# A fused attention kernel: order of additions, PSUM tiles and pieces of projection work rearranged

## The chip, the cores and the metric

The kernel runs on one core of a Trainium2 chip. TensorE (PE in the profile) multiplies matrices; PEld is its loading of weights. VectorE (DVE), ScalarE (ACT) and GpSimd (POOL) work on the results, and SyncE (SP) issues DMAs; ScalarE and GpSimd can issue some as well. Each engine takes its own instructions in order. The metric is device time in microseconds, and less is better. Times inside a run come from one profiled execution, counted from its first instruction.

## The reference

The input x holds 16 images of 256 channels and 32 x 32 pixels, so 1024 tokens of 256 channels each, all fp32. Two layers follow each other:

```python
# layer 0: 4 heads of 64
qkv = xs @ w_proj + b_proj                    # xs: 1024 tokens x 256
attn = softmax(q @ k.T * 64 ** -0.5)
x = attn @ v @ w_out + b_out + xs
# layer 1: 8 heads of 32
h = group_norm(x, gn1_w, gn1_b)               # 32 groups of 8 channels
attn = softmax(q @ k.T * 32 ** -0.5 + phys_bias)
x = x + attn @ v @ proj_w.T + proj_b
h = group_norm(x, gn2_w, gn2_b)
x = x + mlp_w2 @ gelu(mlp_w1 @ h + mlp_b1) + mlp_b2   # 256 -> 1024 -> 256
```

## The kernel before, in words

Everything is kept as channels x tokens, 128 channels to a tile, and a token block (TB) is 512 tokens. For each image `b` the loop runs the first attention (`attention_a`), then either the first MLP half of the image before (`hidden`, lines 784 to 796) or, for image 0, the q, k and v projections of image 1; then the first part of this image's own projections for the second attention (`qkv_1`), and the second attention (`attention_b`). Into the second attention the remaining work is strewn in pieces: the rest of its own projections (`own`), the second MLP half of the image before (`outputs`), and the q, k and v projections for the next image (`first`). Images 0 and 15 have no `outputs` or no `first`, so they have fewer pieces.

Softmax isn't normalised at once. Scores go from TensorE to PSUM, ScalarE takes their exponentials to SBUF (tiles `e`), TensorE multiplies these with v (`weigh`, tiles `acc`), and VectorE adds the exponentials up (tiles `es`). At the end of an item (a token block and a group of heads) a matmul with ones gives the denominators (`den`), ScalarE copies them out, a DMA spreads them over partitions, VectorE inverts them, two more DMA steps bring them back as rows, and VectorE scales the result. Then the output projection runs, `o` for the first attention and `j` for the second, and its sum with x gets the statistics of the next group norm.

PSUM has eight banks of 128 x 512 fp32. Six make three wide tiles of two banks, s0 to s2, which `wide` (line 232) gives out by least recent use; two are the single banks 0 and 1 (`bank`, line 238). While the first attention works at an odd item, s2 holds its accumulator; the set `kept` then takes s2 out of the rotation. At an even item the accumulator is in banks 0 and 1. In the second attention a unit covers two blocks of 128 keys: the first block's scores go to banks 0 and 1 and one wide tile, the second's to two wide tiles. Bank 0 also takes the unit's `acc`, and once in each image the v projection named `v[1]` (`early`, line 898). Whoever writes a tile next waits until its last reader is done.

The order of work on every engine is fixed when the program is built. A `yield` in an attention ends a step; after each step `run` (line 828) issues the pieces that `fill` names for that step and advances `later`, a list of functions that are due a number of steps on. A scheduler then orders the instructions of each engine; `tc.keep_in_program_order` holds some of them.

The places that the change touches are these. `load_rest` (line 138) issues small loads on SP: `bqk`, the bias of q, k and v, and `pb`, the bias of the second softmax. The first image's q and k projections run as `first_qk` (line 854), named by half of the channels, by k or q, and by token block. `weigh` of the first attention empties an accumulator with a ScalarE copy (L373) and a VectorE addition (L374) and says when s2 returns. `normalise` (line 382) takes a wide tile for `den`. In the second attention `add` issues the additions of `es` (L497), `weigh` empties `acc` by a copy (L520) or an addition (L522), and the loop from line 566 sets their order. `v` of `qkv` empties its tile with a multiply on VectorE (L721). `group_norm` (line 618) has three functions due some steps apart: `means`, `variances` (matmul `gm`) and `apply` (matmul `gv`, then `rstd`, L662, which empties it); norm h is the second one of an image and runs during the first attention of the next.

Of the kernel before, what the change touches and what calls it, by code (L numbers as in the profile page):

```python
# [8 lines left out]
F32 = mybir.dt.float32  # L9
# [5 lines left out]
P = 128  # L15
GROUPS = 32
EPS = 1e-5
HEADS0, D0 = 4, 64
HEADS1, D1 = 8, 32
TB = 512  # L20
# [34 lines left out]
def kernel(  # L55
# [21 lines left out]
    nc = tc.nc  # L77
    B, C, S = x.shape
    HID = mlp_w1T.shape[1]
    CC = C // P  # L80
    SB = S // P
    NT = S // TB
# [54 lines left out]

    def load_rest():
        bp = b_proj.rearrange("(g i t d) -> i t d g", i=2, t=3, d=D0)
        for t in (1, 0):  # L140
            for i in range(2):
                nc.sync.dma_start(bqk[i * D0 : (i + 1) * D0, t, :], bp[i, t])
        nc.sync.dma_start(pb, phys_bias.partition_broadcast(P))
        for i in range(2):
            nc.sync.dma_start(bqk[i * D0 : (i + 1) * D0, 2, :], bp[i, 2])
        for t, w in weights:
            nc.sync.dma_start(t, w)
# [53 lines left out]
def first_pass(ctx, tc, x, out, k):  # L201
# [120 lines left out]
    def attention_a(b, qT, kT, v, project):  # L322
        key, D, lag = f"a_{b}", D0, 2
        items = [(t, c) for t in range(NT) for c in range(CC)]
        units = [(i, kb) for i in range(len(items)) for kb in range(SB)]
        res = act.tile([P, CC, S], F32, tag="res", name=f"res_{key}")
        accs, held, sums = {}, {}, {}

        def scores(i, kb):
            t, c = items[i]  # L330
            if kb == 0 and i % 2:
                kept.add(2)
            s = wide(f"s_{key}_{i}_{kb}")
            for g in range(2):
                for h in range(0, P, HALF):
                    nc.tensor.matmul(  # L336
                        s[h : h + HALF, g, :],
                        kT[g * D : (g + 1) * D, c, kb * P + h : kb * P + h + HALF],
                        qT[g * D : (g + 1) * D, c, t * TB : (t + 1) * TB],
                        start=True,  # L340
                        stop=True,
                    )
            e = work.tile([P, 2, TB], F32, tag="e", name=f"e_{key}_{i}_{kb}", bufs=8)
            nc.scalar.activation(e, s, AF.Exp, scale=float(D) ** -0.5)  # L344
            return i, kb, e

        def weigh(i, kb, e):
            t, c = items[i]
            if kb == 0:
                if i % 2:  # L350
                    acc = wide(f"acc_{key}_{i}", 2)
                    accs[i] = [acc[:, h, :] for h in range(2)]
                else:
                    accs[i] = [bank(f"acc_{key}_{i}_{h}", h) for h in range(2)]
            for h in range(2):
                for g in range(2):
                    nc.tensor.matmul(  # L357
                        accs[i][h][g * D : (g + 1) * D, :],
                        v[h * HALF : (h + 1) * HALF, kb, c * 2 + g],
                        e[h * HALF : (h + 1) * HALF, g, :],  # L360
                        start=(kb == 0),
                        stop=(kb == SB - 1),
                    )
            if kb == 0:
                held[i] = e
                return
            if kb == 1:
                sums[i] = work.tile([P, 2, TB], F32, tag="es", name=f"es_{key}_{i}", bufs=4)
            nc.vector.tensor_add(sums[i], held[i] if kb == 1 else sums[i], e)  # L369
            if kb == SB - 1:  # L370
                r = res[:, c, t * TB : (t + 1) * TB]
                one, two = accs.pop(i)
                nc.scalar.copy(r, one)  # L373
                nc.vector.tensor_add(r, r, two)  # L374
                if i % 2:

                    later.after(2, lambda: kept.discard(2))
                if c == CC - 1:
                    later.after(2 if t < NT - 1 else 1, lambda: normalise(t))


        def normalise(t):
            half = TB // 2
            den = wide(f"den_{key}_{t}")[:, 0, :]
            for c in range(CC):
                for g in range(2):
                    for h in range(2):
                        j = (2 * g + h) * 32
                        nc.tensor.matmul(
                            den[j : j + 32, c * half : (c + 1) * half],  # L390
                            k["ones"][:, :32],
                            sums[t * CC + c][:, g, h * half : (h + 1) * half],
                            start=True,
                            stop=True,
                        )
            denominators(
                f"{key}_{t}", den_copy(f"{key}_{t}", den), CC * TB,
                (2, 5) if t < NT - 1 else (1, 1),
                lambda full: scale(t, full),
            )  # L400

            if t == 0 and handed:
                handed.pop()()

        def scale(t, full):
            r = res[:, :, t * TB : (t + 1) * TB]
            halves = [
                y.rearrange(form, c=CC, h=2)
                for y, form in ((r, "p c (h q) -> p c h q"), (full, "p (h c q) -> p c h q"))
            ]  # L410
            tc.keep_in_program_order(nc.vector.tensor_mul(halves[0], *halves))
            if t == NT - 1:
                later.after(4, lambda: project(t, res)())

        cols[0] = 32
        pending = []
        for n, u in enumerate(units):
            pending.append(scores(*u))
            if n == len(units) - 1:
                break  # L420
            if n >= lag:
                weigh(*pending.pop(0))
            yield
        while pending:
            weigh(*pending.pop(0))
            if not pending:


                cols[0] = P
                first_half = project(0, res)  # L430
                first_half((0,))
                yield
                first_half((1,))
                break
            yield
# [7 lines left out]
    def attention_b(b, qT, kT, v, project):  # L443
# [44 lines left out]
        def add(i, kb, es, block):  # L488
# [6 lines left out]
            for n in range(G // 2):  # L495
                d = sums[i][n]
                ins = nc.vector.tensor_add(d, es[n] if kb == 0 else d, es[2 * block + n])  # L497
                if block:
                    tc.keep_in_program_order(ins)

        def weigh(i, kb, es):
            t, c = items[i]
            acc = bank(f"acc_{key}_{i}_{kb}", 0)
            for m in range(2):
                for g in range(G):
                    nc.tensor.matmul(  # L506
                        acc[g * D : (g + 1) * D, :],
                        v[:, kb + m, c * G + g],
                        es[2 * m + g // 2][:, g % 2, :],
                        start=(m == 0),  # L510
                        stop=(m == 1),
                    )
            if t not in res:
                res[t] = act.tile(
                    [P, CC, TB], F32, tag="res1" if t == NT - 1 else "res",
                    name=f"res_{key}_{t}",
                )
            r = res[t][:, c, :]
            if kb == 0:
                nc.scalar.copy(r, acc)  # L520
            else:
                nc.vector.tensor_add(r, r, acc)  # L522
            if kb == SB - 2:
                later.after(1, lambda: normalise(i, r, i == len(items) - 1))
# [41 lines left out]
        for u in units:  # L566
            now = scores(*u)
            add(*now, 0)
            if pending:
                weigh(*pending)  # L570
            add(*now, 1)
            pending = now
            yield
# [192 lines left out]
    def attention_1(b, qkv_tiles, xb, norm):  # L766
        q, kk, v = qkv_tiles
        stats = small.tile([P, CC, NT, 6], F32, tag="st1", name=f"st1_{b}", bufs=2)

        def project(t, res):  # L770
            return out_proj(
                f"j{b}", k["wpj"],
                lambda kc: res[:, kc, :],
                k["pjb"], xb, t, stats, (lambda: norm(stats)) if t == NT - 1 else None,
            )

        return attention_b(b, q, kk, v, project)
# [73 lines left out]
    xs = {0: load_x(0)}  # L851
    k["load_rest"]()
    tiles0, (first_qk, first_v) = qkv_0(0, xs[0])
    run_pieces(first_qk + first_v)
    k["exp_bias"]()


# [16 lines left out]
    for b in range(B):  # L874
# [34 lines left out]
            now, end = outputs[:5], outputs[5:]  # L909
        if not first:  # L910

            fill = {0: own[:2], 1: own[2:3], 2: own[3:5], 3: own[5:6], 4: own[6:]}
            fill.update({5 + 2 * m: [piece] for m, piece in enumerate(now)})
            now = []

        rest = [[piece] for piece in now]
# [7 lines left out]
        for m, pieces in enumerate(rest):  # L924
# [4 lines left out]
                b, tiles1, xs[b],  # L929
                lambda st, b=b, hn=hn: group_norm(  # L930
                    f"h{b}", xs[b], st, k["g2w"], k["g2b"], "q1", hn,
                    4 if b + 1 < B else 2, b == B - 1,
                ),
            ),
            fill,
# [305 lines left out]
```

## Time and profile before

| | |
|---|---|
| three timed runs, us | 3809.84, 3809.48, 3809.69 (median 3809.69) |
| the profiled run, us | 3809.61 |
| matmul groups, second attention: scores L467, weigh L506 | 535.4 us and 492.1 us busy |
| matmul groups, first attention: scores L336, weigh L357 | 530.9 us and 527.6 us busy |
| additions es_b L497 (all but each item's first) | 768 x 1219 ns |
| exponentials e_b L482 | 1280 x 865 ns in the mean |
| multiply that empties v_b, L721 | 64 x 684 ns |
| granted TensorE clock | 1.000 |

Busy times of different engines overlap, so they don't add up to the span. A line of the timeline gives start, length, engine, source line, operation, output and inputs, shape and count, and in brackets how long the engine had been idle and what ended that. A line of the waits gives who waited for whom, then the total in us, the number of times, and the longest. One fp32 matmul is two records, and matmuls that use different parts of the array start together: four of 128 x 32, or of 64 x 64, or eight of 32 x 64.

### The profile page before, as it was taken

What the parts mean: (1) busy time and instruction counts of PE and PEld (TensorE: products, weight loads), DVE (VectorE), ACT (ScalarE), POOL (GpSimd) and SP (SyncE); (2) the same over time, 40 slices, a digit from 0 to 9 for tenths busy, and PEclk for the clock granted to TensorE, in tenths of its full rate; (3) what the DMA queues carried; (4) which work ended last, traced back from release to release, by engine and by line L of the source; (5) the groups of instructions that cost most, each with busy time, mean ns of one, the idle gap of its engine ahead of it and who ended that gap; (6) DMA issues with size and microseconds to landing.
All of it is one profiled execution on the core that took longest, in us unless ns stands there. A gap on an engine that the chain in (4) does not pass through costs nothing.

```text
span 3807.8 us, 86808 instructions
## 1 busy us (share of the span) xinstructions
PE 3757.8 (99%) x38335; PEld 1490.8 (39%) x38335; DVE 2230.3 (59%) x2764; ACT 2034.1 (53%) x2624; POOL 79.0 (2%) x245
## 2 busy tenths in 40 slices
PE   9999999999999999999999999999999999999999
PEld 4333333333333333333333333333333333333335
DVE  4674646646566465665656656565565655646573
ACT  4555546555465554545546455554555545555462
POOL 1000000000000000000000000000000000000000
PEclk9999999999999999999999999999999999999999
DMA  2000000000001000000000001010000100000000
GB/s 84 12 13 12 30 12 16 27 12 30 12 16 32 7 30 12 19 29 7 30 12 23 25 10 32 7 33 15 13 30 7 33 15 13 30 7 22 15 13 21
DMA packets 63052, 78.27 MB, mean 21 GB/s; under 512 B 35820, under 2 KB 37356, under 8 KB 62668
## 3 DMA queue, kind: packets, MB, share of 16 engines
q1 hardware_dynamic: 60684, 71.85, 6.1%
q8 instruction: 302, 4.95, 0.5%
q0 software_dynamic: 400, 0.41, 0.1%
q14 instruction: 82, 0.67, 0.1%
q10 hardware_dynamic: 1584, 0.39, 0.0%
HBM read 54.28 MB, written 17.56 MB: 19 GB/s over the span
## 4 chain that ended last, share of the span: by engine, by line
PE 94%; DVE 2%; ACT 2%; issue 2%; DMA 0%; ACTq 0%; POOLq 0%; POOL 0%; DVEq 0%
PE s_b L467 13%; PE acc_b L506 12%; PE m L787 12%; PE m L279 12%; PE s_a L336 11%; PE acc_a L357 10%; PE qk_a L279 6%; PE qk_b L279 5%; PE o L279 3%; PE v_a L279 3%; PE j L279 3%; PE v_b L279 2%; PE den_b L531 1%; ACT e_b L482 1%; DVE es_b L497 1%
## 5 line engine op out<-in xcount | busy, mean ns | idle before, releaser
L482 ACT ACTIVATE e_b<-s_b 128x1024 f32<-128x1024 f32 (+1 forms) x1280 | 982.6, 865 | 500.0 <-PE s_b L467 500.0
L497 DVE TENSOR_TENSOR es_b<-es_b,e_b 128x1024 f32<-128x1024 f32 x768 | 899.6, 1219 | 365.6 <-ACT e_b L482 365.6
L344 ACT ACTIVATE e_a<-s_a 128x1024 f32<-128x1024 f32 x512 | 521.0, 1024 | 361.5 <-PE s_a L336 341.5
L467 PE MATMUL s_b<-q,k 32*64 32x512 f32 x8192 | 535.4, 601 | 30.2 <-DVE v L721 24.6
L336 PE MATMUL s_a<-q,k 64*64 64x512 f32 x4096 | 530.9, 592 | 3.3 <-ACT e_a L344 3.3
L357 PE MATMUL acc_a<-e_a,v 64*64 64x512 f32 x4096 | 527.6, 589 | 0.0
L369 DVE TENSOR_TENSOR es_a<-es_a,e_a 128x1024 f32<-128x1024 f32 x384 | 469.0, 1221 | 88.2 <-ACT e_a L344 76.0
L506 PE MATMUL acc_b<-e_b,v 128*32 128x512 f32 x4096 | 492.1, 598 | 0.0
L279 PE MATMUL m<-g,w 128*32 128x256 f32 (+1 forms) x7664 | 464.2, 379 | 0.0
L787 PE MATMUL m<-gn_h,w 128*128 128x512 f32 x1024 | 451.3, 595 | 0.3 <-DVE gn_h L677 0.3
L795 ACT ACTIVATE g<-m,m1b 128x512 f32<-128x512 f32 x256 | 175.9, 687 | 355.3 <-PE m L787 355.3
L279 PEld LDWEIGHTS m<-g,w 128*32 128x32 f32 (+1 forms) x7664 | 276.7, 112 | 217.2 <-issue 42.1
L467 PEld LDWEIGHTS s_b<-q,k 32*64 32x64 f32 x8192 | 172.5, 130 | 317.6 <-issue 149.5
L787 PEld LDWEIGHTS m<-gn_h,w 128*128 128x128 f32 x1024 | 192.2, 190 | 230.6 <-issue 229.8
L357 PEld LDWEIGHTS acc_a<-e_a,v 64*64 64x64 f32 x4096 | 160.1, 133 | 279.3 <-issue 242.4
L336 PEld LDWEIGHTS s_a<-q,k 64*64 64x64 f32 x4096 | 153.1, 133 | 276.8 <-issue 216.2
L506 PEld LDWEIGHTS acc_b<-e_b,v 128*32 128x32 f32 x4096 | 108.5, 109 | 351.6 <-ACT e_b L482 194.7
L522 DVE TENSOR_TENSOR res_b<-res_b,acc_b 128x512 f32<-128x512 f32 x192 | 130.9, 682 | 192.9 <-PE acc_b L506 192.9
L279 PE MATMUL qk_b<-gn_g,wq 128*32 128x512 f32 (+1 forms) x1280 | 234.0, 592 | 0.0
L279 PE MATMUL qk_a<-x,wp 128*32 128x512 f32 (+1 forms) x1856 | 231.0, 592 | 1.1 <-DMA x<-in_x_dram 1.0
L721 DVE TENSOR_TENSOR v<-v_b,eones 128x512 f32<-128x512 f32 x64 | 43.8, 684 | 242.5 <-PE v_b L279 242.5
L497 DVE TENSOR_TENSOR es_b<-e_b,e_b 128x1024 f32<-128x1024 f32 x128 | 150.7, 1219 | 52.4 <-ACT e_b L482 52.4
(121 smaller groups left out, 2095.3 us busy)
## 6 DMA issues: line engine op xcount, KB each, us to landing
rd_a<-row_a SPq DMA_DIRECT2D x64, 256.0 KB
out_dram<-x SPq DMA_DIRECT2D x64, 256.0 KB
rd_b<-row_b SPq DMA_DIRECT2D x252, 64.0 KB
x<-in_x_dram SPq DMA_DIRECT2D x30, 512.0 KB
w<-in_L_conv_mlp_w_dram SPq DMA_DIRECT2D x2, 1024.0 KB
x<-in_x_dram SPq DMA_DIRECT2D x4, 256.0 KB
sp_b<-d_b SPq DMA_DIRECT2D x63, 8.0 KB
row_b<-inv_b SPq DMA_DIRECT2D x63, 8.0 KB
```

The costliest lines, as they stand in the source:

```text
L279: nc.tensor.matmul(o[sl], w[:, sl], r, **flags)
L336: nc.tensor.matmul(s[h : h + HALF, g, :], kT[g * D : (g + 1) * D, c, kb * P + h : kb * P + h + HALF], qT[g * D : (g + 1) * D, c, t * TB : ...
L344: nc.scalar.activation(e, s, AF.Exp, scale=float(D) ** -0.5)
L357: nc.tensor.matmul(accs[i][h][g * D : (g + 1) * D, :], v[h * HALF : (h + 1) * HALF, kb, c * 2 + g], e[h * HALF : (h + 1) * HALF, g, :], st ...
L369: nc.vector.tensor_add(sums[i], held[i] if kb == 1 else sums[i], e)
L467: nc.tensor.matmul(outs[g][h : h + HALF, :], kT[g * D : (g + 1) * D, c, k0 : k0 + HALF], qT[g * D : (g + 1) * D, c, t * TB : (t + 1) * TB] ...
L482: nc.scalar.activation(to, s, AF.Exp, scale=float(D) ** -0.5)
L497: ins = nc.vector.tensor_add(d, es[n] if kb == 0 else d, es[2 * block + n])
L506: nc.tensor.matmul(acc[g * D : (g + 1) * D, :], v[:, kb + m, c * G + g], es[2 * m + g // 2][:, g % 2, :], start=(m == 0), stop=(m == 1),)
L522: nc.vector.tensor_add(r, r, acc)
L787: nc.tensor.matmul(ps, k["w1"][:, cc, hc * P : (hc + 1) * P], hn[0][:, cc, t * TB : (t + 1) * TB], start=(cc == 0), stop=(cc == CC - 1),)
L795: nc.scalar.activation(g, ps, AF.Gelu, bias=k["m1b"][:, hc : hc + 1])
```

## The change

The change has these parts, in the order of the diff:

1. `pb` and the q and k parts of `bqk` are loaded from ScalarE's queue in place of SP's, `pb` first.
2. In the first attention s2 returns to the rotation inside `normalise`, after the denominators have taken their tile; before, it returned two steps after the accumulator was emptied, just ahead of the denominators. After the last item it returns at once. The denominators and the next projection so take each other's tiles.
3. In the second attention the results of image 0 (all but the last token block) lie in the MLP's tiles `g`, and those of image 15 in `q0`, a tile for each.
4. At the first unit of the second attention a `yield` comes between the two calls of `add`, so the pieces of step 0 are issued ahead of the first additions.
5. The first image's projections run with all pieces of the first token block first.
6. In images 0 and 15 `own` is given out one piece to a step, the v pieces first, and the output pieces follow two steps later than before.
7. `variances` of norm h is due after 3 steps in place of 4, except in the last image.

```diff
     def load_rest():
         bp = b_proj.rearrange("(g i t d) -> i t d g", i=2, t=3, d=D0)
+        nc.scalar.dma_start(pb, phys_bias.partition_broadcast(P))
         for t in (1, 0):
             for i in range(2):
-                nc.sync.dma_start(bqk[i * D0 : (i + 1) * D0, t, :], bp[i, t])
-        nc.sync.dma_start(pb, phys_bias.partition_broadcast(P))
+                nc.scalar.dma_start(bqk[i * D0 : (i + 1) * D0, t, :], bp[i, t])
...
                 nc.vector.tensor_add(r, r, two)
-                if i % 2:
-
-                    later.after(2, lambda: kept.discard(2))
+                if i == len(items) - 1:
+                    kept.discard(2)
...
                 lambda full: scale(t, full),
             )
 
+            kept.discard(2)
             if t == 0 and handed:
                 handed.pop()()
...
+        def result(t):
+            if t < NT - 1 and b == 0:
+                return [
+                    work.tile([P, TB], F32, tag="g", name=f"res_{key}_{t}_{c}", bufs=16)
+                    for c in range(CC)
+                ]
+            tag = "res1" if t == NT - 1 else "res" if b < B - 1 else "q0"
+            r = act.tile([P, CC, S if tag == "q0" else TB], F32, tag=tag, name=f"res_{key}_{t}")
+            return [r[:, c, :TB] for c in range(CC)]
...
             add(*now, 0)
-            if pending:
-                weigh(*pending)
+            if not pending:
+
+                yield
+                add(*now, 1)
+                pending = now
+                continue
+            weigh(*pending)
             add(*now, 1)
             pending = now
             yield
...
-    run_pieces(first_qk + first_v)
+
+    run_pieces(first_qk[::2] + first_qk[1::2] + first_v)
...
-            fill = {0: own[:2], 1: own[2:3], 2: own[3:5], 3: own[5:6], 4: own[6:]}
-            fill.update({5 + 2 * m: [piece] for m, piece in enumerate(now)})
+            fill = {m: [piece] for m, piece in enumerate(own[:5:2] + own[1::2] + own[6:])}
+            fill.update({len(own) + 2 * m: [piece] for m, piece in enumerate(now)})
...
-                    4 if b + 1 < B else 2, b == B - 1,
+                    3 if b + 1 < B else 2, b == B - 1,
```

More of the change, by code (lines that the diff above doesn't have):

```diff
@@ L513, in weigh @@
             if t not in res:
[L514 to L518, printed above, removed]
+                res[t] = result(t)
+            r = res[t][c]
             if kb == 0:
@@ L772, in project @@
                 f"j{b}", k["wpj"],
-                lambda kc: res[:, kc, :],
+                lambda kc: res[kc],
                 k["pjb"], xb, t, stats, (lambda: norm(stats)) if t == NT - 1 else None,
```

## The prediction

> **What bounds the kernel now.** I read the page first, then the waits of TensorE alone, then the timeline around each wait.
>
> ```profile
> span 3807.8 us, 86808 instructions
> PE 3757.8 (99%) x38335; PEld 1490.8 (39%) x38335; DVE 2230.3 (59%) x2764; ACT 2034.1 (53%) x2624; POOL 79.0 (2%) x245
> ...
> PE 94%; DVE 2%; ACT 2%; issue 2%; DMA 0%; ACTq 0%; POOLq 0%; POOL 0%; DVEq 0%
> ```
>
> TensorE is the bound: it is busy for 99% of the span and carries 94% of the chain that ended last. Only what shortens its work or its waits counts; vector and scalar work is free as long as nobody waits for it. The diff leaves the matmuls as they are, so the whole question is the waits. The waits of TensorE name them (total us, times, longest):
>
> ```profile
> PE s_b L467 <- DVE v L721: 24.6, 16, 1.5
> PE den_a L389 <- DVE res_a L374: 8.1, 16, 0.8
> PE s_b L467 <- DVE res_b L522: 4.4, 8, 0.9
> PE s_a L336 <- ACT e_a L344: 3.3, 15, 0.2
> ...
> PE s_b L467 <- ACT res_b L520: 1.0, 3, 0.7
> PE qk_a L279 <- DMA x<-in_x_dram: 1.0, 1, 1.0
> ```
>
> The first two come once per image, 16 times in all. These totals are too small: a matmul of 512 columns is shown as 0.59 us long, but the next may start 0.43 us after it (in the undisturbed timeline score and weigh groups start 0.86 us apart, each of two passes of 0.43). So I take waits from start to start. The biggest one, in image 5 (column one is the start, column two the length):
>
> ```profile
> 1270.15 1.93 PE L279 MATMUL v_b<-wq,gn_g 128*32 128x256 f32 x32
> 1271.90 1.90 PE L279 MATMUL qk_b<-gn_g,wq 128*32 128x512 f32 x16
> 1272.32 2.36 DVE L497 TENSOR_TENSOR es_b<-e_b,e_b 128x1024 f32<-128x1024 f32 x2 [3.27 <-ACT e_b L482]
> 1274.60 0.68 DVE L721 TENSOR_TENSOR v<-v_b,eones 128x512 f32<-128x512 f32 x1
> 1275.34 1.98 PE L467 MATMUL s_b<-q,k 32*64 32x512 f32 x32 [1.53 <-DVE v L721]
> ...
> 1280.71 1.90 PE L279 MATMUL qk_b<-gn_g,wq 128*32 128x512 f32 x16
> 1282.54 1.97 PE L467 MATMUL s_b<-q,k 32*64 32x512 f32 x32
> ```
>
> The projection qk_b has four groups of 0.43, so the scores could start at 1271.90 + 1.72 = 1273.62; they start at 1275.34, 1.72 late. They want bank 0, which v_b filled and the multiply L721 must empty; that multiply stands on VectorE behind two additions of 1.2 us, though its input was done at about 1272. The last two lines are the same pair of steps without a wait: 1282.54 against 1280.71 + 1.72 leaves 0.11 us, the price of the switch alone. So 1.72 - 0.11 = 1.61 us per image is wait.
>
> The second wait, in image 6:
>
> ```profile
> 1428.15 1.04 PE L357 MATMUL acc_a<-e_a,v 64*64 64x512 f32 x8
> 1428.93 0.68 DVE L374 TENSOR_TENSOR res_a<-res_a,acc_a 128x512 f32<-128x512 f32 x1
> 1429.67 1.07 PE L389 MATMUL den_a<-es_a,ones 128*32 128x256 f32 x16 [0.48 <-DVE res_a L374]
> 1430.56 3.62 PE L279 MATMUL j<-res_b,wpj 128*32 128x512 f32 x32
> ```
>
> The denominators could start at 1428.15 + 0.86 = 1429.01 and start 0.66 late, when L374 has emptied tile s2; net of the switch 0.55.
>
> **What the Trainium skill says.** "Perfetto Trace Analysis", section Optimization Strategy: a gap that repeats on the engine that should be full can mean that there is no free PSUM tile; both waits are exactly that. The same page, section Matmuls: independent groups should rotate through banks so that emptying one lies beside the next group; here bank 0 is given to v_b and then at once to the scores, and s2 from the accumulator to the denominators. "ScalarE: Activation LUTs", section What ACT_TABLE_LOAD costs, gives 1283 ns and a drain of about 1380 ns; the trace agrees on 1.28 us (10.60 to 11.88), but the first activation follows at 11.89, with no drain between. "DMA: Bandwidth & Descriptors", section Anatomy of one DMA: a DMA's semaphore wait is held by the issuing engine's sequencer. The trace agrees: SP issues its first bqk at 2.87 and its second only at 5.20.
>
> **The change part by part.** The order of the built program is what I follow.
>
> The order on VectorE: in all 16 images the multiply of v_b 1 now stands before the two additions. The cause is the yield between the first scores and their additions. In the 14 middle images nothing else moves there. v_b's last pass starts at about 1271.68; the earlier multiply (v_b 0) began 0.42 after its last pass started, so this one runs from 1272.1 to 1272.8, before 1273.62. The additions then start 0.5 us later than before, at 1272.8, and end at 1275.2; the next additions could then start at 1277.57 - 1.72 = 1275.85, so the delay is absorbed. ScalarE had done the first unit's exponentials by 1273.20 and its k copy runs 1273.87 to 1274.45; the second half of the scores, 1273.73 + 0.86 = 1274.59, is the first to want that tile. Gain 14 x 1.61 = 22.5 us; I allow 20 to 22.5.
>
> In images 0 and 15 one piece per step means that no qk_b lies behind v_b 1. The scores wait for the multiply to end at about 1272.83 in the same clock, where they could start at 1271.90: 0.96 with the switch, against 1.72. Gain 2 x 0.76 = 1.5 (1.0 to 1.8).
>
> Tiles: the denominators take s1 in place of s2 and the projection j takes s2. The last reader of s1, the exponential of the scores before last, ended at 1427.76, before 1429.01; the sums they read were done at 1425.53. The denominators take four passes of 0.215, to about 1429.97 with the switch; j then wants s2, free at 1429.61. No new wait: 16 x 0.55 = 8.8 us (7 to 9.3). At the end of the first attention the denominators take s2 instead of s1; there o lies between, and L374 ended at 1224.92 in the timeline while they start at 1225.39: nothing, hidden by o.
>
> Group norm h, a step earlier in 15 images. Before:
>
> ```profile
> 1443.43 1.22 DVE L369 TENSOR_TENSOR es_a<-es_a,e_a 128x1024 f32<-128x1024 f32 x1
> 1443.96 1.02 ACT L344 ACTIVATE e_a<-s_a 128x1024 f32<-128x1024 f32 x1 [0.69 <-PE s_a L336]
> 1444.57 0.24 PE L630 MATMUL gv_h<-tv_h,gavg 64*64 64x2 f32 x4
> 1445.04 1.09 PE L336 MATMUL s_a<-q,k 64*64 64x512 f32 x8 [0.22 <-ACT e_a L344]
> ```
>
> gv_h took one of two free tiles, so the next scores waited for the exponential that ends at 1444.98; start to start the excess over 0.06 is 0.41. After, gv_h comes before the scores of 1442.80 with three tiles free, and the scores at about 1444.60 take gv_h's own tile. It is emptied by rstd L662, which still stands on VectorE behind the last addition; that can start when its exponential ends (1443.26) and ends at 1444.52, rstd's two halves at 1444.85. So 0.31 of 0.41 comes back under another name: 15 x 0.1 = 1.5 us (0 to 5.3). gm_h comes at 1439.31 instead of 1441.02; its input was written at 1438.26, 1.05 before. Queued behind it on VectorE: mean, dv, tv (0.8 us) now ahead of one addition, which waits for its exponential anyway.
>
> Units without a piece, images 0 and 15: there the scores wait for L520 or L522 to empty bank 0 (lines three and five of the waits). Image 0 gains pieces before units 6 and 7, whose scores were 0.82 and 0.59 late from start to start: minus two switches 1.2. Image 15 gains one before unit 7: 0.59 - 0.11 = 0.5. I take off 0.3 because v_b 3 now stands without qk_b before it. Net 1.4 (0.7 to 1.9). The new result tiles are free when asked for: nothing. On SP one output DMA moves behind later small ones, an issue of some 0.6 us (as the other SP issues take) on an idle queue: nothing.
>
> The start. Before:
>
> ```profile
> 9.71 7.48 PE L279 MATMUL qk_a<-x,wp 128*128 128x512 f32 x16 [1.00 <-DMA x<-in_x_dram]
> 10.60 1.28 ACT L700 ACT_TABLE_LOAD   x1 [10.60 <-DMA bqk<-in_L_conv_b_proj_dram]
> ```
>
> The second projection piece waits 1.17 (8.11 + 0.43 to 9.71) for the second half of x, and the fourth 0.24 for ScalarE. In the new order four pieces use the first half, up to 5.97 + 4 x 1.72 = 12.85, so the 1.17 goes; the q weights that the second piece now wants landed at 8.26, where it needs them at 8.55. But pb and four bqk are now issued by ScalarE's sequencer, ahead of its first activation, and they wait for the three wp and for pb: by SP's issues at 5.20, 6.82 and 8.36 the last goes at about 9.0 and ends at 9.6. Then table 1.28, ebias 0.21, k 0.69: 11.8. The fourth piece wants that tile at 11.13: 0.7 lost. Gain 1.17 + 0.24 - 0.7 = 0.7 (-0.6 to 1.3). SP, freed of five issues, sends the weights earlier; nobody waits for those.
>
> Sum: 22.5 + 1.5 + 8.8 + 1.5 + 1.4 + 0.7 = 36.4 us of the span 3807.8. The three timed runs lie within 0.36 us, 1.9 above that span in the median, so the same difference is taken off 3809.69: 3773.3.
>
> **The rivals.** First: the multiply goes first, but the scores then stand waiting for ScalarE or for a third tile. For it: the k copy clears the tile only 0.14 us before it is wanted. Against: the same pattern runs without a wait at 1282.54. Nothing of 22.5 is gained: 3795.8. Second: the exchange only renames the wait, j waits for s2 in place of the denominators; for that L374 would have to end over 0.36 us later than now. Against: its queue is unchanged. 8.8 lost: 3782.1. Third, the other sign: gm_h, a step earlier, reaches TensorE before VectorE has its mean; in order, TensorE stops with everything behind it. Its slack is 1.05 us. It pays from there on, and to end slower by 0.2% (about the least that a measurement of this kernel can tell from no change, 7.6 us) it must cost (36.4 + 7.6) / 15 = 2.9 us per image, a mean 4 us late; the chain L591, L594, L638 would have to double. Time then 3817.3.
>
> **How the numbers follow.** Forecast 0.82, first rival 0.10, second 0.05, third 0.02, 0.01 for no change at all. Predicted is the likeliest, 3773.3. All upper ends together give 42 us (3767.5), all lower ends 28 (3781.6); with the second rival's edge the range is 3767 to 3783, leaving out the first and third. Faster over 0.2%: 0.82 + 0.10 + 0.05 = 0.97; within 0.01; slower 0.02.
>
> **What would show it.** In the waits of TensorE the v line should shrink from 24.6 to under 2 us (two images), the den_a line vanish, the s_a line stay near its size but name rstd L662. In the chain in order of time the images follow each other every 235.46 us (L787 at 992.92 and at 1228.38); less 1.61, 0.55 and 0.1 that becomes 233.2. The first v_a should come about 0.7 earlier than 21.32. I am wrong if s_b waits for e_b or k L698 in the second unit, if j waits for L374, or if gm_h waits for mean_c.

## The result, and the profile after

The changed kernel takes 3773.88 us in the median of four runs (3773.01 to 3774.09), against 3809.75 (3809.48 to 3809.84) for the kernel before. The ratio is 0.9906, with a 95% interval of 0.9888 to 0.9923. The forecast was 3773.3 us, with a range of 3767 to 3783, so the total was met within 0.6 us. Not all of its terms were: the start of the program went the other way, and images 0 and 15 gave more than forecast. The sections below take them apart.

From the page of the kernel after, whose span is 3772.0 us: busy time by engine, and the chain's shares by engine.

```profile
PE 3757.8 (100%) x38335; PEld 1492.0 (40%) x38335; DVE 2231.3 (59%) x2764; ACT 2034.8 (54%) x2624; POOL 78.5 (2%) x245
...
PE 97%; DVE 1%; issue 1%; ACT 1%; DMA 0%; ACTq 0%; POOLq 0%; POOL 0%; DVEq 0%
```

TensorE is busy for the same 3757.8 us as before and runs the same 38335 matmuls. What went is idle time: its share of the chain rose from 94% to 97%. So the gain is all in waits. These are the waits of TensorE in the kernel after (who waits for whom, total us, times, longest):

```profile
PE s_b L468 <- DVE res_b L532: 3.3, 6, 0.9
PE qk_a L279 <- ACT q L715: 1.5, 1, 1.5
...
```

The 24.6 us on the multiply of v (L721, here L736, because the change moved the lines below it), the 8.1 us of the denominators and the 3.3 us of the first attention's scores on their exponential are gone from this list. In images 0 and 15 part of the first stays under another name, as shown below. New are two waits at the very start, this 1.5 on `q` and another of 0.6 on `k` of image 0; they are taken up below.

The first piece of a middle image's second attention, in the timeline of the kernel after (start, length, engine, line, operation, shape and count):

```profile
1260.42 1.90 PE L279 MATMUL qk_b<-gn_g,wq 128*32 128x512 f32 x16
1260.67 0.69 DVE L736 TENSOR_TENSOR v<-v_b,eones 128x512 f32<-128x512 f32 x1 [3.11 <-PE v_b L279]
1261.28 2.35 DVE L498 TENSOR_TENSOR es_b<-e_b,e_b 128x1024 f32<-128x1024 f32 x2
1262.25 1.97 PE L468 MATMUL s_b<-q,k 32*64 32x512 f32 x32
```

The multiply now starts at 1260.67 and ends at 1261.36, and the two additions come after it. The scores start at 1262.25, which is 1260.42 + 1.72 for qk_b and 0.11 for the switch: no wait is left.

The denominators of the first token block in the first attention, and behind them the projection j that closes the second attention of the image before, same view:

```profile
1415.07 1.04 PE L357 MATMUL acc_a<-e_a,v 64*64 64x512 f32 x8
1415.85 0.68 DVE L374 TENSOR_TENSOR res_a<-res_a,acc_a 128x512 f32<-128x512 f32 x1
1416.03 1.07 PE L388 MATMUL den_a<-es_a,ones 128*32 128x256 f32 x16
1416.92 3.62 PE L279 MATMUL j<-res_b,wpj 128*32 128x512 f32 x32
```

The denominators start 0.96 after the accumulation, that is 0.86 and a switch, while L374 is still at work. The projection j wants the tile that L374 empties; it is free at 1416.53 and j comes at 1416.92. So the second rival, the renamed wait, did not come true.

And norm h, same view:

```profile
1430.13 1.10 PE L357 MATMUL acc_a<-e_a,v 64*64 64x512 f32 x8
1430.92 0.33 DVE L677 TENSOR_SCALAR rstd_h<-gv_h 64x2 f32<-64x2 f32 x2
1431.30 1.09 PE L336 MATMUL s_a<-q,k 64*64 64x512 f32 x8
```

The scores could start at 1430.13 + 0.86 = 1430.99. They start at 1431.30, 0.31 late, 0.05 after the second half of rstd ended. The list of TensorE's matmuls doesn't show this, because the wait stands on the weight load (PEld); the list over all engines has it 15 times, for the scores L336 on rstd L677, with 14.3 us. That is idle time of the weight loads, which overlap the matmuls. The 0.31 from start to start is what the matmuls lose.

The chain in order of time lets me price each stretch. The first MLP half (`m`, line 802, 24 matmuls of 10.30 us in all) starts at 1216.89 us in one image and at 1450.09 in the next. That is a period of 233.20 us, against 235.46 before and a forecast of 233.2. The stretches side by side:

| stretch | before, us | after, us | gain | forecast gain |
|---|---|---|---|---|
| start to the first v_a | 21.48 | 23.64 | -2.16 | +0.7 |
| from there to image 1's first MLP half | 264.79 | 260.47 | +4.32 | 3.0 |
| the 14 images after it | 3296.64 | 3264.75 | +31.89 | 31.6 |
| rest of the span | 224.89 | 223.14 | +1.75 | 1.1 |
| sum | 3807.8 | 3772.0 | +35.8 | 36.4 |

The chain counts v_a from the end of the matmul ahead of it, 0.16 later than the timeline does. The middle is right. The start is wrong by 2.9 us, and images 0 and 15 gave 2.0 more than forecast.

### The profile page after: what moved, and what is told of

It reads as the page before. It is cut to its first block, busy times and chain, and to the rows that moved or that the text cites. A ratio compares the mean times of both kernels' runs of the same rounds, so it can differ in the third digit from the quotient of the medians.

```text
span 3772.0 us, 86793 instructions
## 1 busy us (share of the span) xinstructions
PE 3757.8 (100%) x38335; PEld 1492.0 (40%) x38335; DVE 2231.3 (59%) x2764; ACT 2034.8 (54%) x2624; POOL 78.5 (2%) x245
## 4 chain that ended last, share of the span: by engine, by line
PE 97%; DVE 1%; issue 1%; ACT 1%; DMA 0%; ACTq 0%; POOLq 0%; POOL 0%; DVEq 0%
PE s_b L468 13%; PE acc_b L519 12%; PE m L802 12%; PE m L279 12%; PE s_a L336 12%; PE acc_a L357 11%; PE qk_b L279 6%; PE qk_a L279 6%; PE o L279 3%; PE v_b L279 3%; PE v_a L279 3%; PE j L279 3%; PE den_b L541 1%; PE den_a L388 1%; DVE es_a L369 0%
## 5 line engine op out<-in xcount | busy, mean ns | idle before, releaser
L336 PE MATMUL s_a<-q,k 64*64 64x512 f32 x4096 | 532.6, 593 | 1.1
L336 PEld LDWEIGHTS s_a<-q,k 64*64 64x64 f32 x4096 | 152.6, 133 | 278.1 <-issue 211.7
L736 DVE TENSOR_TENSOR v<-v_b,eones 128x512 f32<-128x512 f32 x64 | 44.0, 688 | 291.2 <-PE v_b L279 291.2
```

What stands on the lines that cost most here:

```text
L336: nc.tensor.matmul(s[h : h + HALF, g, :], kT[g * D : (g + 1) * D, c, kb * P + h : kb * P + h + HALF], qT[g * D : (g + 1) * D, c, t * TB : ...
```

## The experiments

Ten kernels ran. Since the start of the program turned out to vary with where its small loads stand, the table gives the first v_a and the span after it as well: a difference in the last column doesn't come from the start. Medians are of four runs, of 20 for the second row. The intervals of most ratios to the kernel before reach 0.0017 to each side, about 6 us, so variants are told apart by their own runs (lowest to highest) and by the last column.

| kernel | median, us | runs | ratio to before (95%) | first v_a | span after it |
|---|---|---|---|---|---|
| after | 3773.88 | 3773.0 to 3774.1 | 0.9906 (0.9888 to 0.9923) | 23.48 | 3748.6 |
| e1, no yield | 3803.95 | 3801.3 to 3808.7 | 0.9986 (0.9979 to 0.9992) | 23.52 | 3778.1 |
| e2, tiles as before | 3784.74 | 3784.2 to 3786.9 | 0.9936 (0.9920 to 0.9953) | 23.52 | 3758.9 |
| e3, norm at 4 | 3775.33 | 3774.7 to 3777.8 | 0.9912 (0.9895 to 0.9929) | 22.85 | 3749.9 |
| e4, loads on SP | 3771.59 | 3771.5 to 3771.7 | 0.9900 (0.9883 to 0.9916) | 21.35 | 3748.5 |
| e5, yield alone on before | 3784.17 | 3783.9 to 3784.6 | 0.9933 (0.9917 to 0.9950) | 21.36 | 3760.9 |
| e6, pieces as before | 3777.05 | 3775.2 to 3780.6 | 0.9915 (0.9898 to 0.9931) | 26.42 | 3750.2 |
| e9, old order, loads on SP | 3771.60 | 3771.4 to 3771.7 | 0.9900 (0.9883 to 0.9916) | 21.19 | 3748.6 |
| e7, gv in s2, loads on SP | 3767.11 | 3767.0 to 3767.3 | 0.9888 (0.9872 to 0.9905) | 21.33 | 3744.05 |
| e10, e7 and table early | 3767.49 | 3766.3 to 3767.6 | 0.9888 (0.9872 to 0.9905) | 21.46 | 3744.1 |

The tenth, e11, stands at the end of this section; it took 4177.23 us. The kernel before has 21.32 and 3786.5 in the last two columns.

**The yield.** e1 takes only the yield out of the kernel after; e5 puts only the yield into the kernel before.

```diff
-            if not pending:
-
-                yield
-                add(*now, 1)
-                pending = now
-                continue
-            weigh(*pending)
+            if pending:
+                weigh(*pending)
```

> The changed kernel without the yield between the first scores and their additions; all else kept. If the multiply that empties v_b 1 stood in the way only because of the two additions ahead of it, its wait returns: 14 x 1.61 us in the middle images, and in images 0 and 15, where no qk_b lies behind v_b 1 any more, about 3.4 instead of 0.96 us each, so 22.5 + 4.9 = 27 us more, 3801; TensorE's waits name DVE v again, 16 times. Rival: other parts of the change (tiles, norm) had opened the room and the yield adds little: under 8 us more, under 3782.

> The kernel before with one part of the change alone, the yield between the first scores and their additions. If the parts are independent, the wait behind v_b 1 goes in all 16 images (a qk_b still lies behind v_b 1 in images 0 and 15): 16 x 1.61 = 25.8 us, 3784. Rival: without the other tiles the next wait takes part of it, more than 3790.

The waits of TensorE in e1:

```profile
PE s_b L468 <- DVE v L731: 27.4, 18, 2.2
```

The wait is back. Behind the start e1 is 29.5 us longer than the kernel after, and its period is 234.80, which is 14 x 1.60 = 22.4 in the middle images. The rest, 7.1, is in images 0 and 15, where the single piece per step leaves nothing to hide the multiply, so that the wait comes twice (18 times for 16 images). About 3.4 of the 7.1 is no wait: behind the longest one, 2.24 us, TensorE ran at half its clock for a while in both images, which cost 1.7 us each time (last section). The expectation didn't have that. On the kernel before, the yield alone gives 25.6 us behind the start, and the line of v is gone from the list of waits, while the others stay at the totals they had (8.1 us for the denominators, 4.4 for L522, 3.3 for the first attention's scores).

So the yield is worth 25.6 alone and 29.5 beside the other parts. That says that part 6 needs part 4. The kernel before without its denominator and norm waits would have 3786.5 - 8.9 - 1.4 = 3776.2 us behind the start; e1, which differs from that by the new order of the pieces, has 3778.1. Without the yield, one piece to a step cost 1.9 us where it was to save; by this sum it did so through the 3.4 us of the lower clock, as the waits alone would have saved 1.5.

**The tiles.** e2 gives s2 back as the kernel before does.

```diff
-                if i == len(items) - 1:
-                    kept.discard(2)
+                if i % 2:
+
+                    later.after(2, lambda: kept.discard(2))
...
-
-            kept.discard(2)
```

> The changed kernel with s2 given back as before, two steps after the odd item's accumulator is emptied, so that the denominators take s2 and the projection j another tile. If the exchange removed a wait of 0.55 us in every image, it costs 16 x 0.55 = 8.8 us: 3782.7, and TensorE waits for DVE res_a in front of den_a again. Rival: the wait had only moved to j or to the scores, so the time stays within 1 us of 3773.9.

Of its waits of TensorE, one is the denominators' on L374 (7.8 us, 16 times), and this is the next:

```profile
PE s_a L336 <- ACT e_a L344: 3.3, 15, 0.2
```

Behind the start it costs 10.3 us: 16 x 0.555 = 8.9 for the denominators, and 1.4 that I had put down to part 7. With the old tiles, the scores behind gv_h wait 0.405 for the exponential again, as before, although gv_h itself still comes a step earlier. So the early norm needs the new rotation; I take the reason to be that the number of free tiles at gv_h depends on which tile the denominators took.

**The norm.** e3 sets the delay of norm h back to 4.

```diff
-                    3 if b + 1 < B else 2, b == B - 1,
+                    4 if b + 1 < B else 2, b == B - 1,
```

> The changed kernel with the second norm's averages due after 4 steps as before. Theory: the wait at gv_h was 0.41 us with the exponential as its end and is 0.31 us with rstd as its end, so 15 x 0.1 = 1.5 us more: 3775.4, and TensorE's waits show s_a behind ACT e_a again. Rival: the earlier step had taken the wait away as a whole, 15 x 0.41 = 6 us more: 3780.

It costs 1.4 us behind the start (its start was 0.6 shorter in the profiled run). That is 15 times the 0.1 between 0.41 and 0.31. In e3's waits of TensorE the scores of the first attention stand with 3.3 us on their exponential again, 15 times. So the earlier norm changed the name of the wait, as forecast, and little more.

**The start.** e4 issues `bqk` and `pb` from SP again, `bqk` first, as before; everything else stays. e9 is e4 with the old order of the first projections.

```diff
-        nc.scalar.dma_start(pb, phys_bias.partition_broadcast(P))
         for t in (1, 0):
             for i in range(2):
-                nc.scalar.dma_start(bqk[i * D0 : (i + 1) * D0, t, :], bp[i, t])
+                nc.sync.dma_start(bqk[i * D0 : (i + 1) * D0, t, :], bp[i, t])
+        nc.sync.dma_start(pb, phys_bias.partition_broadcast(P))
```

```diff
-    run_pieces(first_qk[::2] + first_qk[1::2] + first_v)
+    run_pieces(first_qk + first_v)
```

> The changed kernel with pb and the q and k parts of bqk issued by SP again, in the order of before; the new order of the first projections is kept. Theory: the 2.3 us that the first v_a came later (23.64 against 21.32) are due to the loads on ScalarE's queue, which hold its first activation and land late; with SP the new order alone gains the wait for the second half of x, the first v_a comes at about 20 to 20.5 and the time is 3.2 to 3.6 us less: about 3770.5. Rival: the new order itself is what waits (q weights or k's tile are wanted earlier), and the time stays within 1 us of 3773.9.

> The changed kernel with the start of before as a whole: pb and bqk issued by SP, the first projections in the old order. Theory: the new order is worth the waits of 1.17 and 0.24 us less the 0.64 that the fourth piece waits for k's tile with SP's loads, 0.8 us: the time is 0.8 us over the run with loads on SP and the new order (3771.6), 3772.4. Rival: the new order is worth nothing or costs time, 3771.6 or less.

First the start of the kernel after, in the timeline:

```profile
13.02 1.98 PE L279 MATMUL qk_a<-x,wp 128*128 128x512 f32 x4 [0.61 <-ACT k L715]
...
15.76 0.69 ACT L715 ACTIVATE q<-qk_a,bqk 128x512 f32<-128x512 f32 x1 [2.80 <-DMA bqk<-in_L_conv_b_proj_dram]
...
16.50 5.85 PE L279 MATMUL qk_a<-x,wp 128*128 128x512 f32 x13 [1.50 <-ACT q L715]
```

ScalarE's sequencer is busy with the four `bqk` from 4.82 to 10.84, so the table load comes at 10.88 and k is late by 0.61. Then `q` has to wait for its own bias, and TensorE for `q`, 1.50. The chain of the kernel after shows that bias:

```profile
10.23 5.43 DMA bqk<-in_L_conv_b_proj_dram
```

It was issued at 10.23 and landed at 15.66. In e4 there is no such wait:

```profile
12.66 8.85 PE L279 MATMUL qk_a<-x,wp 128*128 128x512 f32 x20 [0.47 <-ACT k L715]
```

From 12.66 on TensorE runs through. The first v_a comes 2.13 us earlier, at 21.35, where the kernel before has it at 21.32; the span behind it is the same within 0.1. So the move of the loads to ScalarE, with their new order, cost 2.1 us, and e4 beats the kernel after by that alone. The expectation had a first v_a at 20 to 20.5 and 3.2 to 3.6 us less; the part that failed to come is the gain of the new order of projections. In e9 the old order ends at the same place, 21.19: with `bqk` on SP both orders stop at the same gate, the tile of k, which ScalarE can't empty before the bias has landed (e4's table load waits for it until 10.63) and the table load and k's copy are through. What the new order saves by not waiting for the second half of x it gives up there. With these loads, part 5 is worth nothing, and my 1.17 was no gain.

**The pieces.** e6 gives out the pieces of images 0 and 15 as before.

```diff
-            fill = {m: [piece] for m, piece in enumerate(own[:5:2] + own[1::2] + own[6:])}
-            fill.update({len(own) + 2 * m: [piece] for m, piece in enumerate(now)})
+            fill = {0: own[:2], 1: own[2:3], 2: own[3:5], 3: own[5:6], 4: own[6:]}
+            fill.update({5 + 2 * m: [piece] for m, piece in enumerate(now)})
```

> The changed kernel with the pieces of images 0 and 15 given out as before, two at steps 0 and 2. My forecast had the one piece to a step worth 1.4 us and lost 2 x 0.85 behind v_b 1 as against a qk_b there. So the two parts nearly cancel: 0.85 x 2 gained, 1.2 + 0.5 lost, 2 x 0.26 (v_b 3, seen in the changed trace) gained back: 3773.4, within 1 us of the changed kernel. Rival: the spread of the pieces is worth having by itself, more than 1.5 us slower than the changed kernel.

Its median is 3.2 us above the kernel after, but the profiled run lost 2.9 us in its start, where the code is that of the kernel after. Behind the first v_a it costs 1.6 us. The first theory allowed 1, the rival began at 1.5: the pieces are worth more than the forecast gave them. The next part takes them unit by unit; the 0.26 that the expectation read for v_b 3 is too small as well.

**Two ways on from there.** e7 is e4 with gv_h in tile s2 of its own choice, and applied a step later, so that the scores no longer take the tile that rstd must empty.

```diff
-        def averages(name, src):
-            ps = wide(name)
+        def averages(name, src, n=None):
+            ps = wide(name, n)
...
-            later.after(1 if cols[0] == P else 2, apply)
+            later.after(1 if cols[0] == P else 3, apply)
...
-            for sl, ps in averages(f"gv_{key}", st["tv"]):
+            for sl, ps in averages(f"gv_{key}", st["tv"], None if cols[0] == P else 2):
```

> Loads on SP, and the average gv_h of the second norm put into tile s2, which is kept for an accumulator that is first written two steps later; it comes one step later, ahead of the scores that waited. Theory: the wait of 0.31 us for rstd falls out in 15 images, since the scores then take a tile that nobody holds: 15 x 0.31 = 4.6 us under the run with loads on SP, 3767.0. Rival: the scores wait again for the exponential (0.41 as before) or the accumulator waits for rstd, and the time is 3771.6 or more.

The timeline of e7 just after gv_h, whose matmuls start at 1427.31:

```profile
1427.38 1.07 PE L336 MATMUL s_a<-q,k 64*64 64x512 f32 x6
1427.57 0.33 DVE L677 TENSOR_SCALAR rstd_h<-gv_h 64x2 f32<-64x2 f32 x2 [0.33 <-PE gv_h L645]
```

The scores follow gv_h at once and start before rstd does. Behind the start e7 is 4.4 us shorter than e4, where 15 x 0.31 = 4.65 was to be had. This confirms that the 0.31 was a wait for the tile. At 3767.11 us it is the fastest version: 6.8 us below the kernel after and 42.5 below the kernel before.

e10 adds to e7 an activation on a constant before everything else, so that the table load comes at 2.80.

```diff
+    early = const.tile([P, CC], F32, name="early")
+    nc.scalar.activation(early, mhalf, AF.Exp)
```

> As the run with gv_h in s2 and loads on SP, and one tiny exponential of a constant goes first on ScalarE, so that its table load of 1.28 us no longer stands behind the landing of bqk. Theory: k's tile is emptied 1.28 us earlier and the wait of 0.64 us in front of the fourth projection piece falls out: 3767.1 - 0.6 = 3766.5. Rival: there the wp or x landing is what ends last, and nothing changes: 3767.1 within 0.2.

It gains nothing in the median: 3767.49, first v_a at 21.46. TensorE waits 1.1 us for the weights wp at the start; e7's profile has that same wait, so the table load was not what bounded its start. The landing of wp differs from run to run, though. In the profiled run of e11, whose start is that of e10, TensorE waits for neither and the first v_a comes at 20.86, 0.49 earlier than in e4, where it waited 0.47 for `k`. So the early table may be worth half a microsecond when the weights are in time; one of e10's four runs, 3766.27, fits that, but it wasn't tested.

e11 adds to e10 another order of scores: in each unit the block that uses only wide tiles first, and the one that uses banks 0 and 1 second, so that bank 0 has more time to be emptied.

```diff
-            es = []
-            for m in range(2):
+            found = {}
+            for m in (1, 0):
+                es = found[m] = []
...
-            return i, kb, es
+            return i, kb, found[0] + found[1]
```

> As the run with the early table, and in every unit of the second attention the scores of the second block of keys (two wide tiles) go first, those of the first block (banks 0 and 1) after them, so that bank 0 has 0.86 us more to be emptied. Theory: what is left of the waits for bank 0 falls out, 0.34 to 1.07 us six times in image 0 and 0.58 twice in image 15, some 4.5 us, and 0.85 twice behind v_b 1: 6 us, 3760.5. In the middle images nothing changes. Rival: the second pair of wide tiles is then wanted before its exponentials are done and a wait comes into all units: at 0.1 us in 256 units 25 us more, over 3780.

It takes 4177.23 us, a ratio of 1.0964 (1.0946 to 1.0982). The rival said over 3780, but by a wait for the wide tiles; neither theory had what came. In its waits of TensorE acc_b now stands for the exponentials 238 times, with 353.9 us, and v_b 16 times, with 26.6. One place of it in the timeline:

```profile
1486.13 3.83 ACT L486 ACTIVATE e_b<-s_b 128x1024 f32<-128x1024 f32 x5 [5.11 <-PE s_b L471]
1488.62 1.92 PE L522 MATMUL acc_b<-e_b,v 128*32 128x512 f32 x16 [1.66 <-ACT e_b L486]
```

Bank 0 has a second user: the accumulation that follows the scores takes it too. In the old order its exponential is the first on ScalarE; now two wide ones go ahead of it. The one of 512 columns that empties bank 0 ends at 1488.56, acc_b starts at 1488.62, and TensorE has stood 1.66. The slack given to one user of the bank was taken from the next, 238 times in the run.

## Why the prediction was right, and where it was wrong

**The order on VectorE: right.** The forecast was 22.5 us in the middle images from one start-to-start difference of 1.61. e1's period differs from the kernel after's by 1.60. The step that carried it was to measure from start to start: the list of waits gave 24.6 for all 16, the run with the yield alone gave 25.6 (e5). The first rival, a wait for ScalarE in its place, is excluded by the timeline at 1262.25.

**Tiles and norm: right in sum.** The denominators' 0.55 and the norm's 0.1 were met (0.555 and 0.09). That 0.31 would come back as rstd was right, and e7 shows it by taking it away. What I had not seen is that the norm's 0.1 depends on the new tiles (e2).

**The third rival** needed the mean 4 us late. TensorE's list of waits has no line for gm_h, and the period of 233.20 leaves no room for one.

**The start: wrong.** I forecast a gain of 0.7 and the kernel lost 2.2. Four assumptions of that step failed. First, "the last goes at about 9.0 and ends at 9.6": it was issued at 10.23, and the table load came at 10.88. Second, I followed only the issue of the loads and never asked when the last one lands. It took 5.43 us, and `q` needed it. Third, "SP, freed of five issues, sends the weights earlier; nobody waits for those": nobody waits for the weights, but the bias may have to compete with them. The Trainium skill, "DMA: Bandwidth & Descriptors", section "Issuing engines are not separate DMA queues", says that DMAs issued by ScalarE, SP or GpSimd end up on the same 16 DMA engines and interleave. SP had issued 1 MB of wo and wq by 9.86, ahead of the bias, and 2.25 MB more by 12.55, and between 10.2 and 15.7 us these engines were busy for 87%. That the weights slowed the bias is not shown: a bqk that SP issued took 5.34 us in the kernel before (from 5.20) and 5.97 in e4 (from 4.60), with wo and wq not yet issued, while the last one for `q` in e4, issued at 8.5, had landed when `q` ran at 12.51. e4 shows that the queue and the order of the loads are the cause of the 2.1 us; how much of it is the late issue and how much the slow landing was not separated. Fourth, the 1.17 credited to the new order was worth nothing (e9): a wait removed ahead of a later gate is not a gain.

**Units without a piece: mis-sized, twice.** I forecast 1.2 in image 0 and 0.5 in image 15 for pieces put before the scores, and took off 0.3 for both v_b 3; the two images gained about 2.0 more than forecast. The kernel before, TensorE alone, at a unit of image 0 without a piece:

```profile
158.94 1.92 PE L506 MATMUL acc_b<-e_b,v 128*32 128x512 f32 x16
160.80 1.07 PE L467 MATMUL s_b<-q,k 32*64 32x512 f32 x2
162.53 1.97 PE L467 MATMUL s_b<-q,k 32*64 32x512 f32 x30 [0.66 <-ACT res_b L520]
164.43 1.92 PE L506 MATMUL acc_b<-e_b,v 128*32 128x512 f32 x16
```

The kernel after at the same unit:

```profile
157.44 1.92 PE L519 MATMUL acc_b<-e_b,v 128*32 128x512 f32 x16
159.18 1.90 PE L279 MATMUL qk_b<-gn_g,wq 128*32 128x512 f32 x16
...
162.93 1.92 PE L519 MATMUL acc_b<-e_b,v 128*32 128x512 f32 x16
```

From acc_b to acc_b it is 5.49 us both times, though the second has a projection of 1.72 us in it. I had read the wait as 0.82. But the first two records of the scores, which don't wait for bank 0, start at 160.80, and all the others only at 162.53: the real wait is 1.73, the whole piece. A group whose first matmul is free to run hides its wait from whoever counts that matmul as work done in time. So a projection of q or k there costs nothing.

Undisturbed, scores take 1.90 us to the acc_b behind them (162.53 to 164.43). Against that, three units in a row of image 0 were late in the kernel before: the scores at 160.80, 166.28 and 171.53, by 1.73, 1.50 and 1.99. In the kernel after only the last of the three is, by 1.76 (at 170.25); later units are late in both kernels alike. That is a gain of 3.46 where 1.2 was forecast; in image 15 it is 1.7 where 0.5 was.

The other way went v_b 3, which now has no qk_b beside it. The kernel after, all engines:

```profile
140.75 1.91 PE L279 MATMUL v_b<-wq,gn_g 128*32 128x256 f32 x32
142.59 3.11 PE L468 MATMUL s_b<-q,k 32*64 32x512 f32 x32
143.88 0.68 DVE L736 TENSOR_TENSOR v<-v_b,eones 128x512 f32<-128x512 f32 x1
144.61 0.21 PEld L468 LDWEIGHTS s_b<-q,k 32*64 32x64 f32 x8 [0.96 <-DVE v L736]
```

The last scores of the group wait until the multiply has emptied v_b's tile, so acc_b comes at 145.63, 3.04 after 142.59. In the kernel before this takes 1.90 (145.24 to 147.14). So 1.14 is lost in each of the two images, where 0.3 was taken off for both. The wait stands on the weight loads, so TensorE's list of matmul waits doesn't have it. What I took off for v_b 1 in image 0 was right: its scores take 2.85 from 129.58, 0.89 more than they could, where 0.85 was forecast.

For image 0 the sum is 3.46 + 0.72 (v_b 1, 1.61 less 0.89) - 1.14 = 3.04. With 1.2 for its stretch's two waits of denominators and 0.1 for the norm that is 4.3, all of the 4.32 in the table. Nothing is left there for part 3, the tiles of the results, which had no run of its own. In image 15 the same terms give 1.3 of the 1.75; the rest comes in the last output pieces and was not followed.

That the total was met within 0.6 us is in part luck: 2.9 us too many for the start and 2.0 us too few for images 0 and 15 stand against each other.

## What to carry to other kernels

Where one engine is full, price a wait from start to start of its instructions, check that the first record of a group isn't one that was free to run early, and ask for the waits of the weight loads as well as those of the matmuls. When loads are moved to another queue, follow each to its landing and to its reader, and ask what now goes ahead of it; an early part of the program may have a later gate that makes a saved wait worthless. When a PSUM bank is given more time for one user, list all users of that bank in order: the time comes from the next one.

## What the runs showed of the hardware

After a pause of TensorE of 2.2 to 2.5 us its granted clock fell to half for about 3.4 us, from 0.9 to 1.4 us after work began again. In the start of e6, timeline and then windows (stretch, length, busy time and count of PE, PEld, DVE, ACT and POOL, granted clock, DMA share, GB/s):

```profile
17.75 8.83 PE L279 MATMUL qk_a<-x,wp 128*128 128x512 f32 x16 [2.46 <-ACT q L715]
```

```profile
19.00:23.00 4.00, 4.00 (x7) 1.55 (x6) 0.00 (x0) 0.69 (x1) 0.00 (x0) 0.57 1.08 382
```

The same 16 matmuls take 8.83 us from 17.75 here and 7.13 from 16.50 in the kernel after, where the pause was 1.50 and the clock stayed at 1.00. The clock was 0.50 from 19.5 to 22 us; 0.57 over these 4 us is a loss of 0.43 x 4 = 1.7 us, so half the clock for 3.4. In e1, after 2.24 us of waiting for v in image 0, the clock was 0.94 over 130 to 135 us and 0.65 over 135 to 139, and a group of acc_b took 3.14 in place of 1.92; after the same wait in image 15 it was 0.63 over 3622 to 3625 us and 0.80 over 3625 to 3628. Each is 1.7 us lost again. So these three pauses cost another 1.7 us on top of themselves, while the 238 waits of acc_b in e11, 1.66 us and less, left its mean clock at 1.000. Where between 1.66 and 2.24 the limit lies, or what else it depends on, no run shows. The Trainium skill, "TensorE: Matmul & The Clock Gate", Part 1, puts the fall to half rate after an idle window of about 3.4 us that runs freely; in these traces pauses of 2.24 and 2.46 us were enough. It also fits that the four runs of e4, e7 and e9, with the loads on SP, lie within 0.3 us of each other (0.7 in e5, 1.0 in e11, 1.3 in e10), while e2, e3 and e6, where ScalarE issues them and TensorE waits for `q`, scatter by 2.7 to 5.3. The kernel after, with the same start, scattered by only 1.1, and that the clock is the reason was not tried.
